# A graph-network and mixture-of-experts block on one core: output rows stored tile by tile, and the order of stores and additions at the end

## The chip, the core and the metric

The kernel runs on one core of one Trainium2 chip. The metric is the device time of one launch in microseconds. Before the change the median of 3 runs is 177.84 us (177.75 to 177.97).

A core has five instruction streams: TensorE (PE, with its weight loads PEld), VectorE (DVE), ScalarE (ACT), GpSimd (POOL) and SyncE (SP, which here only issues DMAs). DMAs are issued by ACT, SP and POOL; in the profile these issues are named ACTq, SPq and POOLq.

## What is computed

`x` has 1250 rows of 512. Two residual blocks follow each other: a graph convolution with a three-layer decoder over all rows, then a top-2 mixture of 8 experts over the first 512 rows.

```python
def gcn_conv(x, W, b): # edges sorted by destination, self loops added
    h = x @ W.T
    return segment_sum(h[s] * (dinv[s] * dinv[d])[:, None], d) + b

h = relu(gcn_conv(layernorm(x), W1, b1))
z = gcn_conv(h, W2, b2)
y = relu(z @ Wd1.T + bd1)
y = relu(y @ Wd2.T + bd2)
x = x + (y @ Wd3.T + bd3)

for e in range(8): # the FFN, on xg: rows of layernorm(x), gathered by expert
    y_e = gelu(xg @ w1[e]) @ w2[e]
x[:512] += sum over the two chosen experts of weight * y_e
```

Everything is float32 outside; there are T = 512 tokens, two experts to each. All 1250 rows are output: rows 0 to 511 need both blocks, rows 512 to 1249 only the first.

## The kernel before

The 1250 rows are ten tiles of up to 128 rows (`NT = 10`; tile 9 has 98 rows). `xs` holds all of them in on-chip memory, 512 floats to a row; the first four tiles (`TT = 4`) are the tokens of the mixture. For the decoder's first two layers the rows are also three chunks: c0 is tiles 0 to 3, c1 tiles 4 to 7, c2 tiles 8 and 9 (226 rows).

The function `sorted_path` writes every instruction in an order made by hand, and each engine runs its own instructions in that order. Its stages: load, layer norm and first product; edge counts as one-hot products; both graph layers; decoder of chunk 0 and the second layer norm; experts; and the end, which is what the change touches.

The decoder has three steps. `decode1` (line 1078) makes one product on TensorE (L1080) and one ACT activation (L1082). `decode2` (line 1084) makes two products (L1088) from that activation's output, and two activations (L1091). `decode3` (line 1093) makes a tile's final product (L1097: two matmuls in the program, four in the trace's count, 128 x 512), adds it to `xs` on VectorE (L1104) and, for tiles 4 to 9, stores the tile to `out` from ACT's queue (L1106).

The experts' results go to rows of a DRAM buffer, `results_d`, by ten indirect DMAs on GpSimd (L1221). Its first 512 rows hold each token's result of the lower-numbered of its two experts, the next 512 that of the higher. `add_results` (line 1235) loads them on SP's queue (L1240), 512 KB to a DMA: two loads of lower results into `x2`, two of higher results into `got`. The lists `wanted[0]` to `wanted[3]` name these four loads in that order; lower results can be loaded before the last scatter, higher results can't.

A wait on another DMA is added by `behind(ins, ins0, ...)` (line 698): `ins` isn't issued until `ins0` has landed. In `decode3` the stores of tiles 6 to 9 are put behind `wanted[-1]`, the last load of higher results; the stores of tiles 4 and 5 wait only for their additions.

At the end (lines 1327 to 1348) the order is: the four result loads on SP; `decode3` of tile 4; `decode1` of c2; `decode3` of tile 5; `decode2` of c2; `decode3` of tile 6; the four additions of lower results (`add(0, t)`, L1330); `decode3` of tiles 7, 8, 9; the four additions of higher results (`add(1, t)`, L1330). Tiles 0 and 1 are stored by one DMA of 512 KB on ACT's queue, tiles 2 and 3 by one on SP's (L1345). After that each engine reads a flag (L31) and skips a general path (L32), and SP waits until all DMAs have landed.

Of the kernel before, what the change touches and what calls it, by code (L numbers as in the profile page):

```python
# [15 lines left out]
P = 128  # L16
# [3 lines left out]
def kernel(tc, *args):  # L20

    nc = tc.nc
    with tc.tile_pool(name="flag", bufs=1) as pool:
        flag = pool.tile([1, 1], I32, name="flag")
        earlier = sorted_path(tc, flag, *args)  # L30
        missed = nc.values_load(flag[0:1, 0:1], min_val=0, max_val=1)  # L31
        with tc.If(missed == 1):  # L32
            general_path(tc, earlier, *args)
# [15 lines left out]
def sorted_path(  # L49
# [28 lines left out]
    nc = tc.nc  # L78
# [6 lines left out]
    NT = (N + P - 1) // P  # L85
# [3 lines left out]
    TT = TOK // P  # L89
# [11 lines left out]
    def rows(t):  # L101
        return min(P, N - t * P)
# [27 lines left out]
    def bank(name):  # L130
        return mixed.tile([P, 512], F32, tag="mixed", name=name)
# [27 lines left out]
    xs = big.tile([P, NT, D], F32)  # L159
# [3 lines left out]
    def load_x(t, q):  # L163
        return q.dma_start(out=xs[: rows(t), t, :], in_=x[t * P : t * P + rows(t)]).ins
# [76 lines left out]
    for c in range(2):  # L241
# [18 lines left out]
        for a, to in ((dst, dg), (src, sg)):  # L260
            gathers.append(
                nc.gpsimd.indirect_dma_start(
                    out=to[:, c, :],
                    out_offset=None,
                    in_=a.rearrange("(o e) -> o e", o=1),
# [4 lines left out]
    for t in range(SOON, NT):  # L270
        ins = load_x(t, nc.sync)
# [409 lines left out]
    def column(a, n, name):  # L681
# [13 lines left out]
        out=bd3s, in_=bass.AP(tensor=bd3.tensor, offset=bd3.offset, ap=[[0, P], [1, D]])  # L695
    )

    def behind(ins, ins0, reason):
        tc.add_manual_dep(
            ins,  # L700
            ins0.name,
            mybir.DependencyInfo(mybir.DependencyClass.Sync, mybir.DependencyReason.DATA),
            reason=reason,
        )
# [317 lines left out]
    c0, c1, c2 = chunks  # L1022
# [55 lines left out]
    def decode1(c, w):  # L1078
        p1 = bank(f"pd1_{c}")
        nc.tensor.matmul(p1[:, :w], Wd1s, z[c][:, :w], start=True, stop=True)  # L1080
        y1[c] = work.tile([P, 512], F32, tag="y1", name=f"y1_{c}")
        nc.scalar.activation(y1[c][:, :w], p1[:, :w], AF.Relu, bias=bias1)  # L1082

    def decode2(c, w):
        y2[c] = post.tile([P, K2, 512], F32, tag=f"y2_{c}", name=f"y2_{c}")
        for k in range(K2):
            p2 = bank(f"pd2_{c}_{k}")
            nc.tensor.matmul(  # L1088
                p2[:, :w], Wd2s[:, k * P : (k + 1) * P], y1[c][:, :w], start=True, stop=True
            )  # L1090
            nc.scalar.activation(y2[c][:, k, :w], p2[:, :w], AF.Relu, bias=bd2s[k])  # L1091

    def decode3(c, t):
        r = rows(t)
        p3 = bank(f"pd3_{t}")
        for k in range(K2):
            nc.tensor.matmul(  # L1097
                p3[:r],
                y2[c][:, k, t * P - c : t * P - c + r],
                Wd3s[:, k, :],  # L1100
                start=(k == 0),
                stop=(k == K2 - 1),
            )
        nc.vector.tensor_add(xs[:r, t, :], p3[:r], xs[:r, t, :])  # L1104
        if t >= TT:
            ins = nc.scalar.dma_start(out=out[t * P : t * P + r, :], in_=xs[:r, t, :]).ins  # L1106
            if t > TT + 1:
                behind(ins, wanted[-1], "behind rows that are wanted sooner")


    x2 = post.tile([P, TT, D], F32)
# [120 lines left out]
    wanted = []  # L1232
# [35 lines left out]
    for t in range(TT):  # L1268
        decode3(0, t)
        second_stats(t)  # L1270
        if t:
            second_norm(t - 1)
        if t == 1:
            decode1(*c1)
# [54 lines left out]
    def add(k, t):  # L1329
        nc.vector.tensor_add(xs[:, t, :], xs[:, t, :], got[k][:, t, :])  # L1330

    decode3(c1[0], TT)
    decode1(*c2)
    decode3(c1[0], TT + 1)
    decode2(*c2)
    for t in range(TT + 2, NT):
        decode3(c1[0] if t < 2 * TT else c2[0], t)
        if t == TT + 2:
            for i in range(TT):
                add(0, i)  # L1340
    for t in range(TT):
        add(1, t)
        if t % 2:
            q = nc.sync if t > 2 else nc.scalar
            q.dma_start(  # L1345
                out=out[(t - 1) * P : (t + 1) * P, :].rearrange("(t p) d -> p t d", p=P),
                in_=xs[:, t - 1 : t + 1, :],
            )
    return []
@with_exitstack  # L1350
def general_path(
# [398 lines left out]
```

## Time and profile before

| what | value |
|---|---|
| median of 3 runs | 177.84 us (177.75 to 177.97) |
| the profiled execution | 174.7 us |
| its span, first to last instruction | 173.0 us |
| busy: PE, PEld, DVE, ACT, POOL | 138.8, 98.8, 99.1, 69.0, 104.2 us |
| mean granted TensorE clock | 0.973 |
| HBM read, written | 18.52 MB, 8.33 MB |
| output stores | 5 of 256 KB and 1 of 196 KB (L1106), 2 of 512 KB (L1345) |

The profile is one execution, recorded by the hardware profiler. Times of an instruction count from the span's start. The span leaves out what lies around it (174.7 against 173.0). A busy share over the whole span says little about the end; for that the timeline and the short windows of the trace are to be read. In timelines a row gives start, duration, engine, line, operation, the tiles written and read, a count, and in brackets the idle time ahead of it with what ended it. In windows a row gives the stretch, its length, each engine's busy time with its count, the granted TensorE clock as a share of full speed, the busy share of the 16 DMA engines and what they moved. A DMA issue's row is short: the transfer itself comes after it.

### The profile page before, as it was taken

How to read it: one execution, taken by the hardware profiler on the slowest of the kernel's cores; microseconds unless marked ns; L12 is line 12 of the kernel's file. 1: busy time of each engine (PE TensorE's matmuls, PEld its weight loads, DVE VectorE, ACT ScalarE, POOL GpSimd, SP SyncE). 2: the span in 40 equal slices, each digit the busy share in tenths (PEclk: the TensorE clock that was granted, in tenths of full speed). 3: DMA queues.
4: the chain of work that ended last, by engine and by line, in shares of the span. 5: the costliest groups of instructions: out<-in, count | busy, mean ns of one | idle time of the engine just before them, and what ended most of it. 6: DMA issues, size and time to landing. Idle time of an engine off the chain costs nothing.

```text
span 173.0 us, 3268 instructions
## 1 busy us (share of the span) xinstructions
PE 138.8 (80%) x1236; PEld 98.8 (57%) x1236; DVE 99.1 (57%) x180; ACT 69.0 (40%) x154; POOL 104.2 (60%) x168
## 2 busy tenths in 40 slices
PE   0059746979989889899999999998899999999100
PEld 0049636866659789685334479685729954454000
DVE  5789999994999999604496731231013101229800
ACT  3077587899725546442131484132212212120000
POOL 8589889998999999999993004674242004600000
PEclk9999999999999999999999999999999999999955
DMA  5978510201853654530000142799988602479382
GB/s 157 311 171 313 154 66 0 7 0 18 262 133 107 202 166 169 198 121 4 0 0 0 61 155 67 209 301 325 383 319 257 237 0 77 168 229 398 110 328 89
DMA packets 18333, 27.12 MB, mean 157 GB/s; under 512 B 4280, under 2 KB 9145, under 8 KB 18312
## 3 DMA queue, kind: packets, MB, share of 16 engines
q1 hardware_dynamic: 15460, 19.34, 35.0%
q0 software_dynamic: 1712, 5.41, 9.5%
q10 hardware_dynamic: 1140, 2.10, 3.4%
q8 instruction: 11, 0.18, 0.5%
q14 instruction: 10, 0.08, 0.3%
HBM read 18.52 MB, written 8.33 MB: 155 GB/s over the span
## 4 chain that ended last, share of the span: by engine, by line
PE 50%; DVE 22%; ACT 8%; DMA 7%; issue 6%; POOL 2%; ACTq 1%; DVEq 0%; POOLq 0%
PE pd L1097 10%; DVE om L493 9%; PE ey L1212 9%; PE l L560 7%; PE eh L1196 6%; DVE on L493 5%; PE ph L317 4%; DMA xg<-x2d,tokens 4%; PE pf L1179 3%; PE pd L1088 3%; DMA win<-in_dst_dram 3%; PE pt L308 2%; ACT xc L297 2%; POOL xg L1149 2%; PE pd L1080 1%
## 5 line engine op out<-in xcount | busy, mean ns | idle before, releaser
L493 DVE TENSOR_TENSOR om<-iota_m,keys_m 128x4096 f16<-128x4096 f16 (+1 forms) x14 | 29.9, 2138 | 0.0
L1221 POOL DMA_INDIRECT results_d<-y,targets x10 | 9.8, 977 | 24.3 <-ACT y L1217 15.7
L560 PE MATMUL l<-T,hp 128*128 128x192 bf16 (+5 forms) x180 | 20.3, 253 | 0.4 <-DVE hp L448 0.4
L308 PE MATMUL pt<-ident,xc 128*128 128x128 f32 (+1 forms) x40 | 7.1, 312 | 15.1 <-ACT xc L297 15.1
L1212 PE MATMUL ey<-w,hT 128*128 128x512 f32 (+1 forms) x64 | 18.9, 598 | 0.0
L532 ACT CAST T<-acc 128x480 bf16<-128x480 f32 (+1 forms) x27 | 14.7, 545 | 10.6 <-PE acc L524 10.4
L1196 PE MATMUL eh<-xgT,w 128*128 128x160 f32 x128 | 18.6, 300 | 0.0
L1097 PE MATMUL pd<-Wd3s,y 128*128 128x512 f32 (+1 forms) x40 | 18.0, 592 | 0.0
L1149 POOL DMA_INDIRECT xg<-x2d,tokens x9 | 8.7, 967 | 15.1 <-PE pf L1179 12.6
L1196 PEld LDWEIGHTS eh<-xgT,w 128*128 128x128 f32 x128 | 17.6, 190 | 0.2 <-issue 0.2
L560 PEld LDWEIGHTS <-hp 128*128 128x128 bf16 (+1 forms) x216 | 14.9, 97 | 3.6 <-issue 1.4
L521 PE MATMUL acc<-on,om 128*128 128x60 f16 x209 | 15.3, 190 | 0.0
L1219 DVE TENSOR_SCALAR y<-ey,wslot 128x512 f32<-128x512 f32 x5 | 3.8, 750 | 20.1 <-PE ey L1212 18.5
L524 PE MATMUL acc<-on,om 128*128 128x60 f16 x209 | 15.0, 190 | 0.2 <-DVE on L493 0.2
L308 PEld LDWEIGHTS pt<-ident,xc 128*128 128x128 f32 (+1 forms) x40 | 5.2, 161 | 15.8 <-issue 9.6
L493 DVE TENSOR_TENSOR on<-iota_n,keys_n 128x960 f16<-128x960 f16 (+2 forms) x28 | 14.1, 542 | 0.0
L521 PEld LDWEIGHTS <-om 128*128 128x128 f16 x209 | 13.6, 98 | 0.7 <-issue 0.5
L317 PE MATMUL ph<-W1s,xT 128*128 128x128 f32 (+1 forms) x80 | 12.5, 309 | 1.0 <-ACT xT L310 1.0
L524 PEld LDWEIGHTS <-om 128*128 128x128 f16 x209 | 12.7, 97 | 0.2
L1026 POOL TENSOR_TENSOR xs<-xs,bd3s 128x512 f32<-128x512 f32 (+1 forms) x10 | 12.4, 1276 | 0.0
L1097 PEld LDWEIGHTS pd<-Wd3s,y 128*128 128x128 f32 (+1 forms) x40 | 7.5, 188 | 8.2 <-issue 7.7
L1212 PEld LDWEIGHTS ey<-w,hT 128*128 128x128 f32 (+1 forms) x64 | 6.9, 149 | 9.2 <-issue 8.4
(217 smaller groups left out, 279.1 us busy)
## 6 DMA issues: line engine op xcount, KB each, us to landing
w<-in_L_ffn_w_dram SPq DMA_DIRECT2D x16, 512.0 KB
xs<-in_x_dram SPq DMA_DIRECT2D x9, 256.0 KB
results_d<-zero SPq DMA_DIRECT2D x4, 512.0 KB
out_dram<-xs ACTq DMA_DIRECT2D x5, 256.0 KB
x2d<-x SPq DMA_DIRECT2D x4, 256.0 KB
x<-results_d SPq DMA_DIRECT2D x2, 512.0 KB
got<-results_d SPq DMA_DIRECT2D x2, 512.0 KB
win<-in_dst_dram SPq DMA_DIRECT2D x2, 336.0 KB
```

The lines of the kernel that those rows point to most:

```text
L308: nc.tensor.transpose(pt[:, k, :r], xc[:r, k * P : (k + 1) * P], ident[:r, :r])
L317: nc.tensor.matmul(to, xT[:, k, :r], W1s[:, k, :], start=(k == 0), stop=(k == KD - 1))
L493: nc.vector.tensor_tensor(to.rearrange("p j (a f) -> p j a f", f=4), iota.rearrange("p (a f) -> p a f", f=4).unsqueeze(1).broadcast_to([P, ...
L521: nc.tensor.matmul(acc[:, n0 : n0 + NK], om[:, (at + g) * HT, :], on0[:, at + g, :], start=True, stop=False)
L524: nc.tensor.matmul(acc[:, n0 : n0 + NK], om[:, (at + g) * HT + 1, :], on1[:, at + g, :], start=False, stop=True,)
L532: nc.scalar.copy(T[:, :, g0 * GN : (g0 + ng) * GN], acc[:, : ng * NK].rearrange("p (d t) -> p t d", t=NT),).ins
L560: nc.tensor.matmul(ps[row0 : row0 + m, a:b], s[:r, t, :m], moving, start=start and i == 0, stop=stop and i == len(order) - 1,)
L1026: pool.tensor_add(xs[:r, t, :], xs[:r, t, :], bd3s[:r])
L1097: nc.tensor.matmul(p3[:r], y2[c][:, k, t * P - c : t * P - c + r], Wd3s[:, k, :], start=(k == 0), stop=(k == K2 - 1),)
L1149: return pool.indirect_dma_start(out=xg[j], out_offset=None, in_=x2d[:], in_offset=bass.IndirectOffsetOnAxis(ap=tokens[:, j : j + 1], axis=0),
L1196: nc.tensor.matmul(ph[:, f, :], first_w[e][:, k, f * P : (f + 1) * P], xgT[:, k, e, :], start=(k == 0), stop=(k == KD - 1),)
L1212: nc.tensor.matmul(to, hT[e][:, f, a:b], second_w[e][:, f, :], start=(f == 0), stop=(f == KF - 1))
```

## The change

It has three parts. Tiles 0 to 3 are stored one by one, by four DMAs of 256 KB on SP's queue, each right after its tile's last addition. All decoder stores (tiles 4 to 9) are put behind `wanted[1]`, the second load of lower results; before, tiles 4 and 5 had no such wait and tiles 6 to 9 stood behind `wanted[-1]`. The additions are placed between the decoder tiles: two of lower results after tile 5, two after tile 6; two of higher results with their stores after tile 8, two after tile 9. TensorE's instructions keep their order: tile 4, `decode1` of c2, tile 5, `decode2` of c2, tiles 6 to 9.

```diff
@@ decode3
         if t >= TT:
             ins = nc.scalar.dma_start(out=out[t * P : t * P + r, :], in_=xs[:r, t, :]).ins
-            if t > TT + 1:
-                behind(ins, wanted[-1], "behind rows that are wanted sooner")
+            behind(ins, wanted[1], "behind rows that are wanted sooner")
@@ end of sorted_path
     def add(k, t):
         nc.vector.tensor_add(xs[:, t, :], xs[:, t, :], got[k][:, t, :])
 
-    decode3(c1[0], TT)
-    decode1(*c2)
-    decode3(c1[0], TT + 1)
-    decode2(*c2)
-    for t in range(TT + 2, NT):
+    def finish(t):
+        add(1, t)
+        nc.sync.dma_start(out=out[t * P : (t + 1) * P, :], in_=xs[:, t, :])
+
+
+    lower_after = {TT + 1: (0, 1), TT + 2: (2, 3)}
+    higher_after = {TT + 4: (0, 1), TT + 5: (2, 3)}
+    for t in range(TT, NT):
         decode3(c1[0] if t < 2 * TT else c2[0], t)
-        if t == TT + 2:
-            for i in range(TT):
-                add(0, i)
-    for t in range(TT):
-        add(1, t)
-        if t % 2:
-            q = nc.sync if t > 2 else nc.scalar
-            q.dma_start(
-                out=out[(t - 1) * P : (t + 1) * P, :].rearrange("(t p) d -> p t d", p=P),
-                in_=xs[:, t - 1 : t + 1, :],
-            )
+        for i in lower_after.get(t, ()):
+            add(0, i)
+        for i in higher_after.get(t, ()):
+            finish(i)
+        if t == TT:
+            decode1(*c2)
+        elif t == TT + 1:
+            decode2(*c2)
     return []
```

## The prediction

> **What bounds the kernel now.** The change touches only the end of the program, so I read, in this order, the chain of waits from 145 us on, the timeline of the end by engine, the 1 us windows over it, and the landing records of the DMA semaphores (cited as "landed").
>
> The chain says that the end is a run of TensorE matmuls with the last additions behind it:
>
> ```profile
> 153.99 6.88 PE pd L1097 x16
> 160.88 0.02 issue
> 160.90 0.04 DVE xs L1104
> 160.93 0.57 issue
> 161.50 1.30 DVE xs L1330 x2
> ```
>
> It stops at the last addition (163.99), 9.0 us before the span's end at 172.98. What fills those 9 us is in the timeline (start, duration, engine, line; ACTq and SPq are DMA issues):
>
> ```profile
> 151.78 0.91 SPq L1240 DMA_DIRECT2D x<-results_d  x2
> ...
> 151.89 0.40 ACTq L1106 DMA_DIRECT2D out_dram<-xs  x1
> ...
> 152.34 0.45 ACT L1082 ACTIVATE y<-pd,bias 128x226 f32<-128x226 f32 x1 [2.15 <-DVE xs L1104]
> ...
> 157.92 1.29 DVE L1330 TENSOR_TENSOR xs<-xs,x 128x512 f32<-128x512 f32 x2 [0.22 <-DMA x<-results_d]
> ...
> 160.90 0.69 DVE L1104 TENSOR_TENSOR xs<-pd,xs 98x512 f32<-98x512 f32 x1 [0.49 <-PE pd L1097]
> ...
> 162.35 3.84 ACTq L1106 DMA_DIRECT2D out_dram<-xs  x4
> 164.02 0.38 SPq L1345 DMA_DIRECT2D out_dram<-xs  x1
> 166.28 0.56 ACTq L1345 DMA_DIRECT2D out_dram<-xs  x1
> ```
>
> Four decoder stores (tiles 6 to 9) stand on ACT's queue until the last load of higher results, `wanted[-1]`, has landed (162.28), then about 2 MB of output leave in one train. The windows show the hole ahead of it and its end (columns: window, length, PE, PEld, DVE, ACT, POOL, clock, DMA share, GB/s):
>
> ```profile
> 161.00:162.00 1.00, 0.00 (x0) 0.00 (x0) 1.00 (x2) 0.00 (x0) 0.00 (x0) 1.00 0.04 12
> ...
> 163.00:164.00 1.00, 0.00 (x0) 0.00 (x0) 0.99 (x2) 0.00 (x0) 0.00 (x0) 0.89 0.65 248
> ...
> 169.00:170.00 1.00, 0.00 (x0) 0.00 (x0) 0.00 (x0) 0.00 (x0) 0.00 (x0) 0.50 0.61 234
> ```
>
> The last store landed at 170.98; final waits and barriers take 2.0 us more. So the end is DMA bound by a train that starts late; TensorE is done at 160.9. This is what the change could win. The line that decides is another: ACT L1082 began at 152.34 after idling 2.15 us "for DVE xs L1104", whose result it doesn't read. It stood behind the store of tile 4 (151.89), which did wait for that addition. ACT's instructions pass in order, and a store's wait holds the activations after it.
>
> [...] ACT waits 7.56 us on line 1106, from 154.75 until `wanted[-1]` lands. [...] the last matmul ends at 160.86 and the clock record falls to 0.50 at 163.77, 2.9 us later. That matmuls at half clock take twice as long is seen at the start (the same shape, 234 ns each by 3.74/16, then 133 by 1.06/8 with modelled ends, 421 against 272 ns median):
>
> ```profile
> 13.22 3.74 PE L317 MATMUL ph<-W1s,xT 128*128 128x128 f32 x16
> ...
> 27.03 1.06 PE L317 MATMUL ph<-W1s,xT 128*128 128x128 f32 x8
> ```
>
> **The change, part by part.**
>
> *Decoder stores behind `wanted[1]`.* In program order ACT now has: store of tile 4, activation L1082, store of tile 5, both L1091, stores of tiles 6 to 9. The store of tile 4 waited for nothing but its addition; now it waits for `wanted[1]`, the second load of lower results, issued at 152.19 and landed at 157.83. L1082 stands behind it, the four L1088 matmuls behind L1082, and all sixteen remaining L1097 matmuls (tiles 6 to 9) behind those on in-order TensorE. This wait puts TensorE to sleep.
>
> When does `wanted[1]` land then? Before, tile 4's 256 KB store moved between 154.7 and 156.2, taking half of saturated engines (401 to 408 GB/s in those windows). Without it the load lands at most 256 KB / 400 GB/s = 0.64 us sooner, at least 0 (at 154 to 155 the loads didn't fill the engines alone). I take 0.4: 157.4, bounds 157.2 to 157.8.
>
> Then: 0.07 us to the store's issue (the addition waiting on the same landing began 0.09 after it), 0.45 from that issue to L1082 (151.89 to 152.34), 0.73 from L1082 to the first L1088 matmul (152.34 to 153.07). 157.4 + 0.07 + 0.45 + 0.73 = 158.65. Before it was 153.07: TensorE's rest moves by 5.6 us, its end from 160.86 to 166.45 at full clock. If the store's issue takes 1.6 us, as one of the later ones does, add up to 1.2.
>
> *Clock.* TensorE's work ends near 153.1 (tile 5) and returns at 158.65: 5.5 us idle, more than the 2.9 that were enough. [...] The 7.8 us of matmuls (153.07 to 160.86) then start at half clock[...] I take 2.2. Bounds 0 (no throttle) and 3.4.
>
> *Additions between tiles.* Eight L1330 at 0.69 (pitch 0.61), as before. Additions of lower results cost nothing, under 7.8 us of matmuls; without that cover 4 x 0.61. Of the four for higher results, two move ahead of tile 9's addition: the run after the last matmul shrinks from 3.13 us (160.86 to 163.99) to 3.13 - 2 x 0.61 = 1.9. At full clock those two additions reach past the last matmul by some 0.2, so 2.1. Gain 1.0. `got` is there: its last load landed at 162.28, and the additions come later now.
>
> *Stores tile by tile on SP.* The paired stores of 512 KB (one ACT, one SP) become four of 256 KB on SP: four issues of 0.38 instead of two, each waiting for its own addition, beside other work. SP holds nothing else, so no one is queued there. The last bytes are 256 KB in place of a 2 MB backlog: tiles 4 to 8 have 8 us of TensorE time to leave. A lone 256 KB store took, from issue 162.35, 2.0 us until 15 of 16 parts had landed (164.34) and 3.15 to the last (165.50). I take 2.8, with tile 9's and tile 2's stores ahead of it; bounds 2.0 and 3.6. Before, last addition to last landing was 170.98 - 163.99 = 7.0: gain 4.2.
>
> *Sum.* Full clock: 166.45 + 2.1 + 2.8 + 2.0 (final waits) = 173.35 against 172.98, +0.4. With the clock loss +2.6. The profiled execution took 174.7 for its span of 173.0, the runs' median is 177.84, 3.1 above: I carry the difference over, as nothing outside the end changes. 177.84 + 2.6 = 180.4. So a gain of about 5.2 at the end pays for a stall of 5.6, and the clock tips it.
>
> **Rivals.** *B, the clock holds.* Stall and gains as above[...]: +0.4, 178.2. [...] Against: idle is nearly twice what sufficed.
>
> *C, the stall is shorter than the gain (faster).* Without the store the loads might run at 400 GB/s from their first packets near 153: 1 MB by 155.7, landed near 156.4. TensorE restarts a microsecond sooner and at full clock the end comes 0.6 earlier: 177.2. It decides from a landing before about 157.0 with the clock kept. Against: windows at 153 to 155 show 117 and 322 GB/s, before the store's packets mattered.
>
> *D, the change doesn't do what it says:* the wait holds only the DMA and the activation slips past. TensorE ends at 160.9, and 4.6 MB of loads and stores from 153 at 400 GB/s end near 165.5; span about 167.8, 172.7. Against: the 2.15 us of L1082.
>
> **How the numbers follow.** Stall with throttled clock 0.75 (180.4; 178.7 to 181.9 by its bounds), B 0.14, C 0.07, D 0.04. What a measurement here can tell from no change is about 0.2%, 0.36 us. A is slower throughout; B lies on that border: slower 0.07, same 0.05, faster 0.02. So faster 0.13, same 0.05, slower 0.82. The range 177.9 to 181.7 leaves out C, D and some of both tails of A and B, about 0.2.
>
> **What would show it.** Right: TensorE idle about 5.5 us after tile 5, ended by ACT L1082; L1082 near 157.9; tile 4's store issued just before it; a clock record of 0.50 inside the span with L1097 at twice its 0.43 us pitch; the last store issued 2 us behind the last matmul and landed 3 us later. Wrong: L1082 still near 152.3 (D); `wanted[1]` landing before 157 (C); L1097 at 0.43 throughout (B).

## The result, and the profile after

The kernel after took 181.01 us (median of 4 runs, 179.27 to 181.63) beside 177.80 us for the kernel before (median of 4, 177.44 to 177.97): 3.2 us more. The ratio formed with it is 1.0329, 95% interval 1.0243 to 1.0415. A second comparison with many more runs gave 180.82 us (22 runs) beside 178.16 us (40 runs), 2.7 us more, and a ratio of 1.0186 (1.0135 to 1.0238). A ratio is formed from undisturbed runs alone, those not over 1.5% above their kernel's fastest, and as the kernel before scattered from 173.58 to 181.30 us over those 40 runs, few of its runs stay in.

The forecast was 180.4 us, 2.6 us more than before. The direction was right; the size was right by the difference of the medians, and less than half of what the first ratio says (3.29% of 177.8 is 5.8 us). The experiments below settle which of the two is the change's own.

The profiled execution of the kernel after took 180.82 us (span 179.0, mean clock 0.965), 6.1 us more than that of the kernel before (174.7, span 173.0). Not all of that lies at the end. The last scatter of expert results, a POOL instruction at the point where the end that the change touches begins, was issued at 153.06 here and at 150.47 before. So I read every run by its *end stretch*: from the issue of the last scatter to the span's end. It was 22.51 us before and 25.94 us after: 3.4 us more. The other 2.6 us came earlier in the program, where both kernels have the same instructions.

The timeline of the kernel after from the last scatter on (start, duration, engine, line, operation):

```profile
153.06 0.97 POOL L1220 DMA_INDIRECT results_d<-y,targets  x1 [0.64 <-ACT y L1216]
...
154.37 0.91 SPq L1239 DMA_DIRECT2D x<-results_d  x2
...
155.87 0.69 DVE L1104 TENSOR_TENSOR xs<-pd,xs 128x512 f32<-128x512 f32 x1 [1.41 <-PE pd L1097]
...
159.94 0.39 ACTq L1106 DMA_DIRECT2D out_dram<-xs  x1
160.38 0.45 ACT L1082 ACTIVATE y<-pd,bias 128x226 f32<-128x226 f32 x1 [7.59 <-DMA x<-results_d]
...
160.88 1.87 PE L1088 MATMUL pd<-y,Wd2s 128*128 128x226 f32 x4 [5.05 <-ACT y L1082]
...
162.55 9.05 PE L1097 MATMUL pd<-Wd3s,y 128*128 128x512 f32 x16
...
171.23 2.74 SPq L1333 DMA_DIRECT2D out_dram<-xs  x4
...
171.72 0.69 DVE L1104 TENSOR_TENSOR xs<-pd,xs 98x512 f32<-98x512 f32 x1
...
172.32 1.28 DVE L1329 TENSOR_TENSOR xs<-xs,got 128x512 f32<-128x512 f32 x2
```

Line numbers of the end are one lower than before; the single stores of tiles 0 to 3 are L1333. Tile 4's addition ends at 154.46, and its store is issued only at 159.94, just after `wanted[1]` has landed (6.81 us after the last scatter). L1082, which needs nothing of that store, starts 0.44 us behind it, after 7.59 us of idle ACT. The bracket names what ACT waited for: "DMA x<-results_d", data that L1082 doesn't touch. TensorE then starts L1088 after 5.05 us without work. Before, the same bracket of L1082 said 2.15 us and "DVE xs L1104".

The second thing to see is the length of the last L1097 group: 9.05 us for sixteen matmuls that took 7.03 us before, and 1.87 us for the four of L1088 that took 0.93. The two rows of before:

```profile
153.07 0.93 PE L1088 MATMUL pd<-y,Wd2s 128*128 128x226 f32 x4
...
153.83 7.03 PE L1097 MATMUL pd<-Wd3s,y 128*128 128x512 f32 x16
```

The clock record of this profile changes at 26.65, 30.07, 159.77, 166.60 and 176.84. The lengths between, 3.41, 129.71, 6.83 and 10.24 us, are 1, 38, 2 and 3 times 3.41; a stretch of that length between the record's edges is called a window below. The windows of the end (window, length, PE, PEld, DVE, ACT, POOL, clock, DMA share, GB/s) say why the matmuls took longer:

```profile
156.35:159.77 3.42, 0.00 (x0) 0.00 (x0) 1.50 (x3) 0.00 (x0) 0.00 (x0) 1.00 1.01 314
159.77:163.18 3.41, 2.30 (x5) 1.84 (x6) 0.00 (x0) 1.29 (x3) 0.00 (x0) 0.50 1.04 402
163.18:166.60 3.42, 3.42 (x5) 1.33 (x4) 0.40 (x1) 0.06 (x1) 0.00 (x0) 0.50 0.04 12
166.60:170.00 3.40, 3.40 (x9) 1.47 (x8) 2.27 (x5) 0.00 (x0) 0.00 (x0) 1.00 0.30 110
```

A window of 3.42 us without one matmul, then two windows at half clock, then full clock. In the third row TensorE is busy all the time and the view counts five matmuls; in the fourth, in the same time at full clock, nine.

After the last matmul the end is short, as the change's other parts were to make it: last addition at 173.60, last store issued on SP at 173.64 and landed at 176.78, span's end at 179.0.

### The profile page after: what moved, and what is told of

The parts are those of the page before. It is cut to its first block, busy times and chain, and to the rows that moved or that the text cites. A ratio compares the mean times of both kernels' runs of the same rounds, so it can differ in the third digit from the quotient of the medians.

```text
span 179.0 us, 3270 instructions
## 1 busy us (share of the span) xinstructions
PE 143.2 (80%) x1235; PEld 101.1 (56%) x1236; DVE 98.9 (55%) x180; ACT 69.4 (39%) x154; POOL 104.3 (58%) x168
## 3 DMA queue, kind: packets, MB, share of 16 engines
q10 hardware_dynamic: 868, 1.58, 2.4%
## 5 line engine op out<-in xcount | busy, mean ns | idle before, releaser
L1097 PE MATMUL pd<-Wd3s,y 128*128 128x512 f32 (+1 forms) x40 | 20.0, 647 | 0.0
L521 PE MATMUL acc<-on,om 128*128 128x60 f16 x209 | 15.7, 191 | 0.1
L524 PE MATMUL acc<-on,om 128*128 128x60 f16 x209 | 15.4, 191 | 0.4 <-DVE on L493 0.4
L521 PEld LDWEIGHTS <-om 128*128 128x128 f16 x209 | 13.9, 99 | 1.2 <-issue 0.8
L1104 DVE TENSOR_TENSOR xs<-pd,xs 128x512 f32<-128x512 f32 (+1 forms) x10 | 6.9, 691 | 13.6 <-PE pd L1097 13.4
L317 PE MATMUL ph<-W1s,xT 128*128 128x128 f32 (+1 forms) x80 | 13.0, 318 | 1.3 <-ACT xT L310 1.3
L1097 PEld LDWEIGHTS pd<-Wd3s,y 128*128 128x128 f32 (+1 forms) x40 | 8.4, 209 | 9.6 <-issue 9.0
L524 PEld LDWEIGHTS <-om 128*128 128x128 f16 x209 | 13.0, 98 | 0.3 <-issue 0.2
L317 PEld LDWEIGHTS ph<-W1s,xT 128*128 128x128 f32 (+1 forms) x80 | 11.9, 228 | 1.7 <-ACT xT L310 1.7
```

Of the source, the lines that this page charges most:

```text
L317: nc.tensor.matmul(to, xT[:, k, :r], W1s[:, k, :], start=(k == 0), stop=(k == KD - 1))
L521: nc.tensor.matmul(acc[:, n0 : n0 + NK], om[:, (at + g) * HT, :], on0[:, at + g, :], start=True, stop=False)
L524: nc.tensor.matmul(acc[:, n0 : n0 + NK], om[:, (at + g) * HT + 1, :], on1[:, at + g, :], start=False, stop=True,)
L1097: nc.tensor.matmul(p3[:r], y2[c][:, k, t * P - c : t * P - c + r], Wd3s[:, k, :], start=(k == 0), stop=(k == K2 - 1),)
```

## The experiments

All times are compared with the kernel before, run beside each experiment; the end stretch is read from each one's profile. In the diffs "-" and "+" are against the kernel named.

### Is it the place of the wait on ACT's queue?

E1, against the kernel after: tiles 4 and 5 are stored without the new wait, all else stays.

```diff
-            behind(ins, wanted[1], "behind rows that are wanted sooner")
+            if t > TT + 1:
+                behind(ins, wanted[1], "behind rows that are wanted sooner")
```

> The changed kernel, with the stores of tiles 4 and 5 again waiting for their additions alone; all else of the change stays (tiles 6 to 9 behind the second load of lower results, tile-by-tile stores on SP, additions between tiles). To be free of what differs ahead of the end, I read the end stretch: from the issue of the last scatter to the span's end, 22.5 us before (150.47 to 172.98), 25.9 changed (153.06 to 178.97). Stall theory (the wait on tile 4's store holds the ACT activation behind it, and TensorE behind that): L1082 about 1.9 us after the last scatter as before, no gap on TensorE, clock 1.00 until its end, end stretch 18 us, median some 4.5 us under before's. Rival (the single-tile stores or the additions cost the time): end stretch stays over 22.5.

E2, against the kernel after: all six stores keep the wait, but those of tiles 4 and 5 are issued after `decode2` of c2, so that no activation stands behind them.

```diff
-        if t >= TT:
-            ins = nc.scalar.dma_start(out=out[t * P : t * P + r, :], in_=xs[:r, t, :]).ins
-            behind(ins, wanted[1], "behind rows that are wanted sooner")
+        if t > TT + 1:
+            store_lower(t)
+
+    def store_lower(t): # the same store and the same wait
...
             decode2(*c2)
+            store_lower(TT)
+            store_lower(TT + 1)
```

> The changed kernel with every wait kept, but the stores of tiles 4 and 5 stand behind decode2's activations in ACT's order, in place of ahead of them. Stall theory (order on ACT alone): L1082 waits only for its product, no gap on TensorE, end stretch 18 us, median some 4.5 us under before's. Rival (it is the wait as such, later stores and a fuller DMA queue, wherever it stands): end stretch near 25.9, as changed.

Measured: E1 175.88 us (22 runs) beside 177.32, ratio 0.9869 (0.9814 to 0.9923), end stretch 20.19. E2 174.73 us (6 runs), ratio 0.9778 (0.9665 to 0.989), end stretch 19.69. The timeline of E2:

```profile
155.19 0.45 ACT L1082 ACTIVATE y<-pd,bias 128x226 f32<-128x226 f32 x1 [1.36 <-PE pd L1097]
...
157.46 7.03 PE L1097 MATMUL pd<-Wd3s,y 128*128 128x512 f32 x16
...
160.55 5.14 ACTq L1110 DMA_DIRECT2D out_dram<-xs  x6
```

L1082 now starts right behind the product that it reads: L1080 ends at 155.15 (the bracket names another matmul of that moment, L1097). The six stores still wait for the same load, which lands at 160.49; their train starts at 160.55. So the cost was never the wait as such; it was that activations stood behind it, L1082 and the two of L1091. E2 has every wait of the kernel after and is some 3% faster than it. Both stretches are about 2 us longer than expected: I had priced the end by TensorE, but with the stall gone the loads and stores, some 4.6 MB, decide, as rival D had it: in E2 TensorE is done at 164.49, 9.3 us before the span's end, and in E8 (below), where it is done at 164.74, the 16 DMA engines are busy for 0.95 from 166 to 167 and for 1.04 from 168 to 170, at 383 and 393 GB/s.

### What is each part worth alone?

E4, against the kernel before: only the wait is changed, for all six decoder stores. Order of additions and stores as before.

```diff
-            if t > TT + 1:
-                behind(ins, wanted[-1], "behind rows that are wanted sooner")
+            behind(ins, wanted[1], "behind rows that are wanted sooner")
```

> The kernel before with one edit of the change: all decoder stores behind the second load of lower results. The old ending stays (four additions of lower results after tile 6, four of higher ones after tile 9, paired stores on ACT and SP). Stall theory: gap of 5 us on TensorE ended by L1082, half clock behind it, and the longer run of additions and two 512 KB stores at the end: end stretch 22.5 + 5.2 + 2.9 less what the stores of tiles 4 to 8 no longer leave for the end, 27.6; median 5 us over before's. Rival (this wait is free, the other two parts cost 3.4): end stretch 22.5.

E8, against the kernel before: one word. Tiles 6 to 9 wait for `wanted[1]` in place of the last load; tiles 4 and 5 stay free.

```diff
-                behind(ins, wanted[-1], "behind rows that are wanted sooner")
+                behind(ins, wanted[1], "behind rows that are wanted sooner")
```

> The kernel before with one word changed: tiles 6 to 9 behind the second load of lower results in place of the last load of higher ones; tiles 4 and 5 free, the old ending. Stall theory: the earlier wait is harmless where no activation stands behind it; tile 6's store leaves near 8 us after the last scatter in place of 11.9: no gap on TensorE, end stretch 20.0. Rival (moving the wait sooner makes stores collide with the loads of higher results and delays their additions): 22.5 or more.

E6, against the kernel after: the waits are those of before; the additions between tiles and the single stores stay.

```diff
-            behind(ins, wanted[1], "behind rows that are wanted sooner")
+            if t > TT + 1:
+                behind(ins, wanted[-1], "behind rows that are wanted sooner")
```

> The changed kernel with the decoder stores' waits as before (tiles 4 and 5 free, tiles 6 to 9 behind the last load of higher results): what is left of the change is the single-tile stores on SP and the additions between tiles. Stall theory: no gap on TensorE, these two parts cost nothing; the train of stores starts at 11 to 12 us after the last scatter and leaves from two queues: end stretch 20.5 against before's 22.5. Rival (these parts cost some of the 3.4 us): over 22.5.

Measured:

| kernel | what of the change it has | median, before beside it | ratio (95%) | end stretch |
|---|---|---|---|---|
| before | nothing | | | 22.51, 22.59 |
| E8 | earlier wait for tiles 6 to 9 | 174.90, 178.16 | 0.9834 (0.9762 to 0.9905) | 19.34 |
| E6 | additions, single stores | 177.56, 178.16 | 1.0041 (0.9942 to 1.0141) | 21.26 |
| E1 | all but the wait of tiles 4 and 5 | 175.88, 177.32 | 0.9869 (0.9814 to 0.9923) | 20.19 |
| E4 | the waits of all six tiles | 179.99, 177.32 | 1.0227 (1.0154 to 1.03) | 25.68 |
| after | everything | 180.82, 178.16 | 1.0186 (1.0135 to 1.0238) | 25.94, 25.61, 25.57 |

Of the two waits that the change makes with one line, that of tiles 6 to 9 gains 3.2 us of stretch (22.51 to 19.34), and that of tiles 4 and 5 costs 5.4 to 5.8 (E1 to the three profiles of the kernel after) or 6.3 (E8 to E4). The two don't simply add: in the kernel after, the wait of tiles 6 to 9 holds nothing any more. Tile 6 is stored at 166.93, right behind its addition, and even the last load of higher results had landed at 162.54. So the 3.2 us belong to an end without the stall. In E8 nothing stalls, and the four stores start 7.81 us after the last scatter (11.88 before):

```profile
156.22 0.45 ACT L1082 ACTIVATE y<-pd,bias 128x226 f32<-128x226 f32 x1 [2.15 <-DVE xs L1104]
...
157.71 7.03 PE L1097 MATMUL pd<-Wd3s,y 128*128 128x512 f32 x16
...
162.15 3.70 ACTq L1106 DMA_DIRECT2D out_dram<-xs  x4
```

E6 gains 1.25 us of stretch (2 were expected); its ratio holds no change. E4 was expected at a longer stretch than the kernel after and came out equal to it. Its TensorE was faster: the last matmul started 16.49 us after the last scatter, 17.94 in the kernel after. The windows of E4 show one at half clock, not two:

```profile
155.85:159.26 3.41, 0.00 (x0) 0.00 (x0) 0.00 (x0) 0.30 (x1) 0.00 (x0) 1.00 1.00 315
159.26:162.67 3.41, 3.21 (x6) 2.18 (x7) 0.00 (x0) 1.05 (x3) 0.00 (x0) 0.50 0.84 320
162.67:166.08 3.41, 3.41 (x9) 1.52 (x8) 2.26 (x4) 0.00 (x0) 0.00 (x0) 1.00 0.28 78
```

In E4 the matmuls came back 0.2 us into a window, which was busy for 3.21 of its 3.41 us, and the clock stood at 1.00 from its end on. In the kernel after they came back 1.1 us into one (busy 2.30), and a second window at half clock followed. Of the 1.45 us by which the last matmuls differ 0.2 is an earlier restart (L1082 at 7.11 us after the last scatter, 7.31 in the kernel after); the rest goes with the one window more at half clock. As E4's stretch is equal all the same, its old ending (additions behind the last tile, paired stores) costs that much more.

### What is the lost clock worth?

E3 and E5, against the kernel after: matmuls that nobody reads fill TensorE's stall, with a bank of their own. E3 has 12 of them, E5 has 6. What `out` gets is unchanged.

```diff
+            warm_bank = bank("warm_bank")
+            for _ in range(6): # E5: range(3)
+                for k in range(K2):
+                    nc.tensor.matmul(
+                        warm_bank, y2[c1[0]][:, k, :P], Wd3s[:, k, :], start=True, stop=True
+                    )
             decode2(*c2)
```

> The changed kernel with twelve matmuls of 128 x 512 added on TensorE between tile 5 and decode2, into a bank that nothing reads: they fill the 5.1 us of the stall and change nothing else. Clock theory (half clock costs 2.9 us of the loss): L1082 as late as in the changed kernel, clock 1.00 up to the last matmul, L1097 at 0.43 us pitch, end stretch 25.9 - 2.9 = 23.0, median about as before's. Rival (the end is bound by the stores, the slow matmuls lie beside them): end stretch 25.9.

> As the run with twelve added matmuls, with six: each is two passes on TensorE, so that twelve took 10.3 us and outlasted the stall of 5.6. Six last 5.2 us, about the stall. Clock theory: L1082 some 7.3 us after the last scatter as in the changed kernel, clock 1.00 up to the last matmul, end stretch 25.9 - 2.9 = 23.1, median about 3 us under the changed kernel's. Rival (the end is bound by the stores, slow matmuls lie beside them): 25.9.

E3 missed its aim: 183.00 us (6 runs), ratio 1.0394 (1.0316 to 1.0473), end stretch 28.42. Each of the twelve is two records in the trace, so they held TensorE for 10.3 us where 5 were to be filled, and L1091 came only 13.48 us after the last scatter. E5 fits the hole:

```profile
153.65 5.31 PE L1350 MATMUL warm_bank<-Wd3s,y 128*128 128x512 f32 x12
...
159.04 0.45 ACT L1082 ACTIVATE y<-pd,bias 128x226 f32<-128x226 f32 x1 [8.27 <-PE warm_bank L1350]
...
159.54 1.03 PE L1088 MATMUL pd<-y,Wd2s 128*128 128x226 f32 x4 [0.58 <-ACT y L1082]
...
160.41 7.03 PE L1097 MATMUL pd<-Wd3s,y 128*128 128x512 f32 x16
```

L1088 takes 1.03 us in place of 1.87 and L1097 7.03 in place of 9.05, and the mean granted clock is 0.989 (0.965 in the kernel after). ACT still idles (8.27 us here), so the stall is there and the clock loss is gone. The bracket of L1082 names the filler, but L1082 starts 0.44 us behind tile 4's store as in the kernel after, and that store was issued at 158.60, just after `wanted[1]` had landed (158.54). From L1082 to the span's end E5 took 15.91 us, the kernel after 18.63, 18.31 and 18.68 in its three profiles: the lost clock was worth 2.4 to 2.8 us. E5's stretch, 23.90, is only 1.7 to 2.0 shorter, because its result loads were issued 2.43 us after the last scatter and not 1.30, for the last but one scatter landed later, so that L1082 came 7.99 us after the last scatter and not 7.31. Its time was 180.05 us (6 runs, 176.67 to 183.12), ratio 1.0111 (1.0015 to 1.0207): 0.8 us under the kernel after, where 3 were expected, a gain within the scatter of six runs. The stretch is the better witness.

### How much of the difference is the end's own?

The kernels before and after once more, as they are, the kernel after twice.

> The changed kernel once more, for how far its times scatter beside those of before on one chip. Clock theory with a window free in phase: the half clock behind the stall lasts one or two windows of 3.41 us, so the end stretch moves between about 24.4 and 26.3 from run to run; L1082 each time about 7.3 us after the last scatter. If the phase were tied to the kernel's start, the stretch would be 25.9 again within 0.3.

> The changed kernel a third time, for the phase of the clock's window alone. Clock theory: end stretch 24.4 to 26.3, by how long the half clock lasts behind the stall; L1082 7.3 us after the last scatter.

> The kernel before once more: end stretch 22.5 within 0.5 whatever the span is; where the span is longer than 173.0, the difference lies ahead of the last scatter (150.5 there), with a record of half clock in its first 35 us.

| profile | time | last scatter | end stretch | clock halved in the front |
|---|---|---|---|---|
| before | 174.70 | 150.47 | 22.51 | no |
| before, again | 178.49 | 154.09 | 22.59 | 25.49 to 28.90 |
| after | 180.82 | 153.06 | 25.94 | 26.65 to 30.07 |
| after, again | 178.44 | 151.10 | 25.61 | no |
| after, third | 180.85 | 153.55 | 25.57 | 26.58 to 30.00 |

The end stretches of one kernel agree within 0.4 us. The half clock of the kernel after lasted two windows in all three profiles, though the matmuls came back 1.1, 2.1 and 1.2 us into one; E4 shows the case with a single window. The issue of the last scatter moves by 3.6 us with the same code. It goes with the clock early in the program. Of all fourteen profiles the four without a halved early window have the last scatter at 150.47 to 151.10, and the ten with one (E8 has two) at 151.85 to 155.70. Here is that stretch in the first profile of before, where the clock held:

```profile
20.41:23.83 3.42, 1.88 (x30) 1.75 (x30) 3.35 (x7) 2.54 (x6) 2.96 (x9) 1.00 0.58 217
23.83:27.24 3.41, 1.80 (x26) 1.67 (x27) 3.41 (x4) 2.75 (x6) 3.16 (x4) 1.00 0.01 2
```

and in its repeat, the same kernel, where it fell:

```profile
22.08:25.49 3.41, 1.30 (x27) 1.17 (x27) 3.34 (x8) 3.08 (x5) 2.84 (x8) 1.00 0.38 142
25.49:28.90 3.41, 2.86 (x27) 2.65 (x26) 3.38 (x5) 2.10 (x5) 3.16 (x6) 0.50 0.00 0
```

TensorE works about half of the time there (1.80 and 1.88 us of a window in the first profile), and what a stretch of 3.41 us holds depends on where its edges lie: in E6, which kept the clock, 1.10 us from 23.00 on and 2.53 from 26.41 on. The window ahead of the fall held 1.09 to 1.64 us of matmuls in all ten profiles that lost the clock; the two windows taken from before held 1.88 and 1.80, the two from E5, which kept it as well, 1.82 and 1.98. One half window can lose at most 1.7 us by itself, an estimate: half of 3.41, as matmuls at half clock took twice their time (1.87 us for L1088 in place of 0.93). What the rest of the 3.6 us is I haven't traced. So the change's own cost is what the end stretches say, 25.57 to 25.94 against 22.51 to 22.59: 3.0 to 3.4 us, 1.7 to 1.9% of 178. That is near both differences of medians (3.2 and 2.7) and agrees with the ratio of the larger comparison. The 5.8 us of the first ratio are outside it, and the 6.1 us between the first two profiles hold 2.6 of the front.

### Can a version beat both?

E9, against the kernel before: E8's one word, and tiles 0 to 3 stored one by one on SP, each right after its last addition; additions in the old order.

```diff
     for t in range(TT):
         add(1, t)
-        if t % 2:
...
+        nc.sync.dma_start(out=out[t * P : (t + 1) * P, :], in_=xs[:, t, :])
```

> The kernel before with tiles 6 to 9 behind the second load of lower results and tiles 0 to 3 stored one by one on SP; tiles 4 and 5 free, the old order of additions (tile 9's ahead of those of higher results). Theory on the additions: without the stall, a wait for higher results ahead of tile 9's addition holds that addition on VectorE's order (12.5 us after the last scatter in the run with tiles 4 and 5 free, 10.4 with the old order), so the old order is the better one: end stretch 19.0, against 20.2 there and 19.3 with paired stores. Rival (the order of additions makes no difference, single stores cost four issues): 20.2.

E10: E9, and the stores of tiles 4 and 5 behind `wanted[1]`, issued after `decode2` of c2 as in E2.

```diff
+    store_lower(TT)
+    store_lower(TT + 1)
```

> As the run before it, with the stores of tiles 4 and 5 put behind decode2's activations and behind the second load of lower results. The loads of results then have the DMA engines alone until they land, about 1 us sooner for the last: higher results are added sooner, no activation waits. End stretch 18.5; median 3.5 to 4 us under before's. Rival (the end is bound by the sum of bytes, 4.6 MB, in whatever order): 19.0 to 19.3.

Measured: E9 175.09 us (22 runs) beside 177.57 (43), ratio 0.9913 (0.9869 to 0.9957), stretch 19.80. E10 174.82 us (23 runs), ratio 0.9825 (0.9782 to 0.9868), stretch 20.58. Both beat both kernels, and neither beats E8, which is one word (174.90, stretch 19.34), or E2 (174.73, 19.69): the four medians lie within 0.4 us. Both miss what was expected of their stretches, 19.0 for E9 and 18.5 for E10. In E10 the loads did land sooner, the last one 10.06 us after the last scatter in place of 11.62, and TensorE had no stall. But the last store landed 18.36 us after the scatter, against 17.58 in E9. It looks as if bytes kept off the loads' way come back behind them; with one profile of each, and E10's the slowest of its 23 runs, the 0.8 us between them are not shown to be the order's, and the medians don't have them. Without the stall, order matters little in these runs: five orders (E1, E2, E8, E9, E10) end within 19.3 to 20.6, with about the same 4.6 MB to move.

## Why the prediction was right in kind, and what it mis-sized

The step that failed is the size of the lost clock: taken at 2.2 us, it measured 2.9 in the kernel after (2.4 and 2.9 in its repeats). The gain from the last addition on was taken at 4.2 us and came to 3.8, with 0.2 more for the final waits. The stall was forecast 0.4 us too long, which hid part of that. So the terms come to 3.4 us where 2.6 were forecast. The 5.8 us of the first ratio are more than all terms hold; the prediction put the scatter of the front at nothing, and that this is the rest is argued below, not shown.

In the terms of the prediction, each as a move against before:

| term | forecast | kernel after | how measured |
|---|---|---|---|
| TensorE restarts later | +5.6 | +5.2 | first L1088 at 7.81 after the last scatter, 2.60 before |
| lost clock | +2.2 | +2.9 | last matmul starts at 17.94, 9.80 before; 8.14 less 5.22 |
| run behind the last matmul | -1.0 | -1.1 | 2.0 (last matmul's end to last addition's), 3.13 before |
| last addition to last landing | -4.2 | -3.8 | 173.60 to 176.78, 7.0 before |
| final waits | 0 | +0.2 | 2.2, 2.0 before |
| sum | +2.6 | +3.4 | stretch 25.94 less 22.51 |

By the same working each of the two repeats comes to a sum of +3.1.

*The wait holds the activation: right.* L1082 started 0.5 us after `wanted[1]` landed, and E1 and E2 take the stall away by the two ways open, no wait or nothing behind it. This rules out rival D (whose sum, besides, has a slip: 4.6 MB at 400 GB/s from 153 on end near 164.5, not 165.5). Of the 0.4 us by which the stall was taken too long 0.2 are the step from L1082 to L1088: 0.73 was read from before, where TensorE was still busy with tile 5 until 153.23; behind the stall it took 0.50. The rest is the load: `wanted[1]` landed 0.55 us sooner than before where 0.4 was forecast, so rival C's mechanism was there, with 0.55 of the 1.4 us that it asked for (157.83 to 156.4).

*The clock: right in kind, and the term that was mis-sized.* The 2.2 us within 0 to 3.4 were the author's estimate. The clock record of before has one change, the fall at 163.77 behind the last matmul, and no return, so it doesn't show for how long matmuls behind a stall run at half clock. Those of E4 and of the kernel after do: in the end's matmuls the clock returned after a window busy for 3.21 of 3.41 us (E4), but not after 2.30 (after), 2.16 (after, third) or 1.30 (after, again). In the kernel after that is 5.7 us of matmuls at half clock, from 160.88 to 166.60, so 2.9 us lost. E5 gives 2.4 to 2.8 for the same by another way. Rival B (the clock holds) didn't happen in any profile of the kernel after. The factor of two for matmuls at half clock was right as well, but its evidence wasn't: no record of that trace shows half clock at the start (the clock records begin at 17.0), and the two rows differ by less than two. The kernel after shows it, 0.85 us from one matmul to the next in place of 0.43.

*Stores and additions: right in kind, 0.5 us too hopeful.* The last store took 3.14 us from issue to landing where 2.8 was taken, within its bounds, and the final waits 0.2 more. The additions between the tiles gave 1.1 us as forecast. But the parts' gains don't stand on their own. The prediction booked 5.2 us of gain to the additions and single stores together; alone (E6) they gave 1.25 of stretch. Against before, most of the gain belonged to a part that the prediction didn't price for itself: tiles 6 to 9 no longer wait for the last load (E8, 3.2). In the kernel after itself no store waits for that load any more: TensorE comes back so late that each of tiles 6 to 9 is stored right behind its own addition. And put on top of E8 the rest gave nothing (E1, 20.19 against 19.34). With the stall gone, an addition between the tiles can itself come too soon. In E1's timeline the first two additions of higher results wait 0.95 us for their load, and tile 9's addition, whose matmuls are long done, comes after them:

```profile
157.67 7.03 PE L1097 MATMUL pd<-Wd3s,y 128*128 128x512 f32 x16
...
165.57 1.29 DVE L1330 TENSOR_TENSOR xs<-xs,got 128x512 f32<-128x512 f32 x2 [0.95 <-DMA got<-results_d]
...
166.78 0.68 DVE L1104 TENSOR_TENSOR xs<-pd,xs 98x512 f32<-98x512 f32 x1
```

It is 12.48 us after the last scatter there, 10.43 in E8. That this makes up the 0.85 us isn't shown: E9, which has the old order of additions and single stores, lies between the two (19.80). In the kernel after the stall itself gave these loads their time.

*The carried difference: right for the median, blind to the scatter.* The prediction took the 3.1 us between the profiled execution (174.7) and the median (177.84) over unchanged, "as nothing outside the end changes". That holds for medians. What the 3.1 us were it didn't ask: scatter of the front, which goes with the early clock window (absent in that one profile, there in before's repeat, which took 178.49). The forecast effect of 2.6 us is smaller than this scatter (3.6 us between two profiles of one kernel). That the first ratio lies so far above what the ends show is most likely its work; that is argued, not shown.

What stays open: why E3 and E5, with matmuls added on TensorE alone, had their last but one scatter land 1.2 us later; what else than the half window holds the front up; and by what rule the clock falls and returns, beyond the windows seen.

## What to carry to other kernels

A wait put on a DMA cost by what stood behind it on the engine that issues it: the wait of tiles 4 and 5 took 6.3 us of stretch ahead of the activations (E4, 25.68, to E8, 19.34), and with the same wait issued behind them the stretch was 19.69 (E2). List those instructions, and who waits for them, before pricing the bytes. If activations stand behind it, move the store behind them in program order (E2) or leave that store unguarded (E8), and keep the wait on the stores that have nothing behind them. When a stall of several microseconds on TensorE can't be avoided, look for half clock behind it and add what the work loses there: here it lasted 3.41 us behind a stall of 4.85 (E4) and 6.83 behind one of 5.05 (the kernel after, which lost 2.9 us by it). And compare kernels by a stretch that starts where their code begins to differ.

## What the runs showed of the hardware

The clock in the end: it returned after windows busy for 3.21 us (E4) and 3.42 (the kernel after), and stayed at half after 1.30, 2.16 and 2.30 (the three profiles of the kernel after). Early in the program it returned after 2.86 (before, again, 25.49 to 28.90). It fell there after windows that held 1.09 to 1.64 us of matmuls, in ten profiles, and not after those of 1.80 to 1.98 in before and E5. The kernel before lost its clock there in one profile (1.30) and kept it in the other (1.88, 1.80), with the same instructions. No single amount of busy time parts all windows seen: in the end of the kernel after the clock didn't fall behind a window of 1.58 (170.01 to 173.43), once it fell after one of 2.58 (E3, 71.42 to 74.83), and in E8's early stretch it didn't return after 3.27 us (26.91 to 30.32) but after the next window's 2.94.

The wait of tile 4's store shows in the profile under another name: ACT's 7.59 us of idle time are booked to the activation behind the store, with the DMA as its releaser. In the waits of the kernel after (waited for: us in total, times, longest) the store's line L1106 isn't what one would look for:

```profile
ACT y L1082 <- DMA x<-results_d: 7.6, 1, 7.6
...
PE pd L1088 <- ACT y L1082: 5.1, 1, 5.1
```

"ACT y L1082 <- DMA" is the sign of it: an activation that waits for a DMA whose data it doesn't read.
